# State-space stage: each unit's preparation issued one unit earlier, its splitting as a separate stream, states multiplied by C in place

## The chip, the cores and the metric

The kernel runs on one core of one Trainium2 chip. The metric is the device time of one execution in microseconds (us). Time before: 5238.29 us, the median of three runs (5235.17 to 5256.56).

The engines that matter here are PE (TensorE, matrix products), DVE (VectorE), ACT (ScalarE, activation functions) and POOL (GpSimd). SP (SyncE) issues nearly all DMA transfers. Each engine works through its own list of instructions in the order in which the program issues them; an instruction that waits for a semaphore holds up all that stand behind it on that engine.

## The reference

A stack of layers works on x of shape (4, 96, 64, 64). Layer 0 is a two-layer Mamba (selective state-space) block on the 4096 positions of each image. Layers 1 to 3 (a bilinear channel mixer, frequency-domain attention and quantised feed-forward layers) follow. The change touches layer 0 alone:

```python
def _mamba_block(seq, ln_g, ln_b, in_w, conv_w, conv_b, xproj_w, dt_w, dt_b, A_log, Dp, out_w):
    mu = seq.mean(-1, keepdims=True)
    var = ((seq - mu) ** 2).mean(-1, keepdims=True)
    h = (seq - mu) * jax.lax.rsqrt(var + EPS) * ln_g + ln_b
    xs, z = jnp.split(h @ in_w, 2, axis=-1)
    xp = jnp.pad(xs, ((0, 0), (DCONV - 1, 0), (0, 0)))
    xc = sum((conv_w[:, k] * xp[:, k:k + L, :] for k in range(DCONV))) + conv_b
    xc = jax.nn.silu(xc)
    dbl = xc @ xproj_w                       # -> dt, Bm, Cm
    delta = jax.nn.softplus(dt @ dt_w + dt_b)
    dA = jnp.exp(delta[..., None] * -jnp.exp(A_log))
    dBx = delta[..., None] * Bm[:, :, None, :] * xc[..., None]
    hstates = jax.lax.associative_scan(comb, (dA, dBx), axis=1)[1]   # h = dA*h + dBx
    y = jnp.einsum('blds,bls->bld', hstates, Cm) + Dp * xc
    return (y * jax.nn.silu(z)) @ out_w
...
for i in range(NLAYERS):                     # 2 layers, C = 96, 192 inner channels, 16 states
    seq = seq + _mamba_block(seq, ...)
```

## The kernel before, in words

`_mamba` (from line 49) computes layer 0. The positions are cut into 8 chunks of 512 (TC). A **unit** is one chunk of one layer for one pair of images, so there are 8 x 2 x 2 = 32 units; they run one after the other, ordered so that a unit's input, made by the layer below, is three units old (two units at the ends are "late": there it is younger). A unit has 24 **steps** (`NS`): three groups k of channels, four r, two halves h. A step scans 4 x 32 rows of 16 states over 512 positions, as two DVE scans of [128, 512].

Per step s, the functions that issue its work are:

- `copies(s)` (L425): a DMA that spreads delta from DRAM (`ddl`) over the states into `a`, six buffers. In 4 of 24 steps, the *apart* ones (steps 2, 6, 10 and 14 of a unit), a second one spreads delta times x into `db`.
- `broadcasts(s)` (L440): PE spreads delta times x over the states into PSUM `pq` (three buffers), from tiles `ux` and `uy`, which hold it split in two parts of fewer bits. In apart steps pq is only a place for the decays.
- `decays(s)` (L449): ACT takes exp of `a` times A, two instructions.
- `product(s)` (L454): times B (`bc`), on DVE in pq; in apart steps on POOL in db.
- `scans(s)` (L459): two DVE scans into `hs`; between them DVE does the product of step s+1. Then POOL multiplies two of the four rows of hs by C into `hc` (on L476). hs and hc have two buffers each, one for two steps (a group g).
- `states(g)` (L478): ACT copies the last column of hs, the state that this unit hands to the next chunk (`hst`).
- `reduce(g)` (L482): PE sums over the states, into `py`.
- `gate` (L492), three times per unit: DVE adds D times x, POOL multiplies by silu(z).

Beside this stream stand generators that prepare and finish units. They are advanced in slots by `Side` (L500): one slot per step (two in a few units), a generator keeps the slot sequence until it yields "free" or "gap", and lanes have an order of rank. `norm` (L189) centres and scales (its reciprocal root is 12 small POOL instructions on tiles `ra` and `r`, its result `hn` is written by DVE). `front` (L252) makes the input projection with the convolution (six matmul groups `mm_i`, one PSUM buffer `mm` for all side work), silu, `mm_dbl` and its split (`dbl`, `dh`, `dx`), the step sizes (`mm_d`, `dl`, softplus), the copy of delta to DRAM, the products `du` = delta times x, and their splitting into ux, uy and ul with DMAs that move quarters between partitions. `tail` (L359) makes the output projection `mm_o` of a finished unit and copies it, as the next layer's input `s` or, for layer 1, as `ft` to DRAM; `rest` (L405) takes the statistics of ft on DVE.

While unit n is scanned, front(n+1) runs as the highest lane from step 0, tail(n-1) is put in line at step 3, norm(n+2) at step 10, and at step 23 what is left is drained:

```python
lanes = (self.front, self.tail, [] if self.tail else self.norm, self.rest)
```

The order of the main loop in each step is: product, broadcasts and decays of an apart step s+2, broadcasts(s+2), reduce of the group that ended two steps before, slots, decays(s+3), scans(s), copies(s+5), states, gate.

Of the kernel before, what the change touches and what calls it, by code (L numbers as in the profile page):

```python
# [48 lines left out]
def _mamba(ctx, tc, io, w, fd, fstats, xsums):  # L49
# [26 lines left out]
    A, HS, HC = ("a", 0, 2, 6), ("hs", 0, 4, 2), ("hc", 0, 4, 2)  # L76
# [12 lines left out]
    out_wT = staged(io["out_wT"], "out_wT", [C, 2, 128], *HC)  # L89
# [12 lines left out]
    dtH = stage("dtH", [128, NL, 256], *HC)  # L102
# [66 lines left out]
    seq, made, ys = {}, {}, {}  # L169
    pqs, das, dbs, hss, hcs, pys = {}, {}, {}, {}, {}, {}  # L170
# [18 lines left out]
    def norm(unit):  # L189
# [47 lines left out]
        for n, b in enumerate(bs):  # L237
# [11 lines left out]
            nc.vector.tensor_tensor(hn_buf[b, l][:C, 3:], p, xc[n], ALU.mult)  # L249
            yield "free"  # L250

    def front(unit):  # L252

        ch, l, pr = unit
        bs = (2 * pr, 2 * pr + 1)
        for j in range(6):
# [13 lines left out]
            if j == 0:  # L270
                xcv = tl("xcv", unit, [128, 3, TC], bufs=2)
            if j == 3:
                zs = tl("zs", unit, [128, 3, TC], bufs=2)
# [32 lines left out]
        bcs = []  # L306
        for k in range(3):
# [8 lines left out]
            if k == 1:  # L316
                for at in range(2):
                    t = tl(f"bc{at}", unit, [128, 2, TC], bufs=2)
                    src = ddb[at].rearrange("s n t -> s (n t)")[:, None].to_broadcast([DS, 8, 2 * TC])
                    nc.sync.dma_start(t.rearrange("p n t -> p (n t)"), src)  # L320
                    bcs.append(t)
# [6 lines left out]
        us, parts, dus, cut = [], [], [], []  # L328
        made[unit] = [xcv, zs, *bcs, dd, us, parts]
        for at in range(6):  # L330
# [6 lines left out]
            for k in ((0, 1), (2,))[at] if at < 2 else ():  # L337
                dus.append(tl(f"du{k}", unit, [128, TC], to="du", bufs=3))
                nc.gpsimd.tensor_tensor(dus[k], dl[:, k, :], xcv[:, k, :], ALU.mult)
# [7 lines left out]
            while at == 3 and side.step < NS * units.index(unit) - 3:  # L347
                yield "gap"
            if 1 <= at < 4:
                cut.append([tl(f"{x}{at}", unit, [128, TC], F32R, to=x, bufs=3) for x in ("ux", "uy")])  # L350
                for t in cut[-1]:
                    nc.scalar.copy(t, dus[at - 1])
# [4 lines left out]
            yield "gap"  # L357

    def tail(unit):  # L359
# [4 lines left out]
        for n in range(2):  # L364
# [13 lines left out]
            else:  # L378
                ft = work.tile([C, TC], F32, name=f"ft_{tag(unit)}_{n}", tag="ft", bufs=2)
# [6 lines left out]
    def way_out(unit):  # L386
# [11 lines left out]
        for n in range(2):  # L398
            b = 2 * pr + n
            nc.vector.bn_stats(fstats[:, b, ch, :], po[:C, n, :])  # L400
            ft = work.tile([C, TC], F32, name=f"ft_{tag(unit)}_{n}", tag="ft", bufs=2)
# [57 lines left out]
    def scans(s):  # L459
# [3 lines left out]
        if h == 0:  # L463
            hss[g] = scan.tile([128, 4, TC], F32, name=f"hs_{name(s)}", tag="hs")
            hcs[g] = scan.tile([128, 4, TC], F32, name=f"hc_{name(s)}", tag="hc")
# [9 lines left out]
        sl = slice(2 * h, 2 * h + 2)  # L475
        (nc.gpsimd if s + 1 < n_steps else nc.vector).tensor_tensor(hcs[g][:, sl, :], hss[g][:, sl, :], bc(unit, 3, k, h), ALU.mult)  # L476

    def states(g):  # L478
        ch, l, pr = steps[2 * g][0]
        nc.scalar.copy(hst[pr, l, g % 12], hss[g][:, :, TC - 1])  # L480

    def reduce(g):  # L482
# [3 lines left out]
        hc = hcs.pop(g)  # L486
# [13 lines left out]
    class Side:  # L500
# [5 lines left out]
        def __init__(self):  # L506
            self.front, self.tail, self.norm, self.rest, self.held, self.step = [], [], [], [], None, 0

        def slot(self):
            waiting = []  # L510
            while True:
                lane = self.held
                if lane is None:
                    lanes = (self.front, self.tail, [] if self.tail else self.norm, self.rest)
# [12 lines left out]

        def drain(self):
# [4 lines left out]
    n_steps = len(steps)  # L533
    with tc.manual_schedule():
# [12 lines left out]
        for s in range(n_steps + NS):  # L547
# [5 lines left out]
            if at == 0:  # L553
                if n + 1 < len(units) and n + 1 not in late:
                    side.front += ([norm(units[n + 1])] if n == 0 else []) + [front(units[n + 1])]
                    side.norm += [weights(1)] * (n == 0)
# [997 lines left out]
```

## Time and profile before

| what | value |
|---|---|
| median of the runs | 5238.29 us (5235.17 to 5256.56) |
| profiled execution | 5239.08 us, span 5237.3 us |
| granted TensorE clock, mean | 0.819 |
| DVE busy over the span | 4322.3 us (83%) |
| PE, ACT, POOL busy | 4069.8, 2693.7, 2988.1 us |
| state-space stage, first to last scan | 93 to 3084 us |
| everything behind it | 3084 to 5237 us |

Busy time is the time in which an engine executes an instruction; waiting isn't counted. A row of the profile by lines gives the line, engine, operation and tiles (out<-in), the count, then busy us and mean ns of one, then the idle time of the engine just before these instructions with what ended it. Who ended a wait is inferred from semaphores; where an instruction waits for several, the name can be that of the wrong one.

### The profile page before, as it was taken

The numbers are of one execution on the slowest core, as the hardware profiler recorded it, in microseconds if no ns is written. First come the engines' busy times: TensorE is split into PE (matmuls) and PEld (weight loads), VectorE is DVE, ScalarE is ACT, GpSimd is POOL, SyncE is SP. The second block draws the span as 40 slices with busy tenths as digits, with TensorE's granted clock in tenths as the row PEclk, the third lists the DMA queues.
The fourth block names the chain that finished last, engine by engine and source line by source line (L and its number), as shares of the span: only waits on it lengthen the run. The fifth ranks groups of instructions, "written<-read, shape, count | busy, mean of one in ns | idle before, by whom it ended". The sixth has DMA issues, their size and how long they took to land.

```text
span 5237.3 us, 52687 instructions
## 1 busy us (share of the span) xinstructions
PE 4069.8 (78%) x15440; PEld 1747.5 (33%) x15440; DVE 4322.3 (83%) x5639; ACT 2693.7 (51%) x5149; POOL 2988.1 (57%) x2105
## 2 busy tenths in 40 slices
PE   5677777777777777777777637899898899989776
PEld 2222222222222222222222102345455555545565
DVE  2879899898989989899998887879787978787655
ACT  3565666656566665656656520024453544434566
POOL 2878888888888888888888860002130312212122
PEclk7767877777787777778787658999999999999977
DMA  4768888888887888888788765553325233332110
GB/s 100 179 168 192 197 193 205 195 197 195 197 195 192 209 196 193 195 197 202 186 208 196 175 168 157 165 174 94 95 86 155 85 98 97 100 90 79 53 33 21
DMA packets 314046, 800.19 MB, mean 153 GB/s; under 512 B 52247, under 2 KB 58106, under 8 KB 312702
## 3 DMA queue, kind: packets, MB, share of 16 engines
q1 hardware_dynamic: 310174, 790.53, 59.8%
q10 hardware_dynamic: 3584, 6.29, 0.4%
q8 instruction: 123, 2.02, 0.2%
q14 instruction: 165, 1.35, 0.1%
HBM read 703.83 MB, written 67.63 MB: 147 GB/s over the span
## 4 chain that ended last, share of the span: by engine, by line
PE 26%; DVE 24%; issue 15%; POOL 11%; ACT 9%; DMA 7%; SPq 1%; DVEq 0%; POOLq 0%; ACTq 0%
DVE hs L470 10%; PE py L895 10%; DVE pq L457 6%; DMA a<-ddl 5%; POOL hc L476 4%; PE py L488 2%; DVE z L880 2%; ACT a L452 2%; DVE a L1110 2%; PE px L1177 2%; PE ph L1092 2%; PE pa L1078 2%; PE mm_i L264 2%; POOL t L1248 1%; PE pv L1133 1%
## 5 line engine op out<-in xcount | busy, mean ns | idle before, releaser
L476 POOL TENSOR_TENSOR hc<-hs,bc 128x1024 f32<-128x1024 f32 x767 | 1803.2, 2360 | 318.4 <-DVE hs L470 305.7
L470 DVE TENSOR_TENSOR_SCAN hs<-a,hst,pq 128x512 f32<-128x512 f32 x1280 | 1575.0, 1263 | 40.1 <-ACT hst L480 17.3
L895 PE MATMUL py<-z,wk 128*96 128x512 f32 x2304 | 1113.1, 612 | 25.0 <-issue 14.0
L452 ACT ACTIVATE a<-a,aneg 128x512 f32<-128x512 f32 x1280 | 846.1, 711 | 223.4 <-DMA a<-ddl 216.1
L880 DVE TENSOR_TENSOR z<-cp,cp 128x512 f32<-128x512 f32 x1152 | 794.9, 717 | 183.7 <-PE py L895 169.0
L457 DVE TENSOR_TENSOR pq<-pq,bc 128x1024 f32<-128x1024 f32 x640 | 773.2, 1208 | 111.6 <-PE pq L447 111.5
L488 PE MATMUL py<-hc,red 128*32 128x512 f32 x3072 | 672.3, 840 | 39.4 <-POOL hc L476 39.4
L895 PEld LDWEIGHTS py<-z,wk 128*96 128x96 f32 x2304 | 366.9, 169 | 448.7 <-issue 318.9
L447 PE MATMUL pq<-uy,sel 64*128 64x512 f32 x768 | 262.9, 643 | 281.1 <-DVE hs L470 275.1
L470 DVE TENSOR_TENSOR_SCAN hs<-pq,hst,db 128x512 f32<-128x512 f32 x256 | 325.5, 1271 | 148.1 <-POOL dx L303 95.0
L1145 POOL MEMSET zz<- 96x2 f32 x16 | 1.6, 98 | 738.5 <-ACT zz L1154 738.5
L264 PE MATMUL mm_i<-hn,wk 97*128 97x512 f32 x512 | 297.7, 710 | 118.3 <-ACT xcv L275 93.2
L1246 POOL TENSOR_TENSOR o<-o,fb 128x384 f16<-128x384 f16 x64 | 67.0, 1047 | 547.1 <-ACT o L1251 544.1
L452 ACT ACTIVATE pq<-a,aneg 128x512 f32<-128x512 f32 x256 | 177.0, 692 | 343.5 <-DMA a<-ddl 249.3
L457 POOL TENSOR_TENSOR db<-db,bc 128x1024 f32<-128x1024 f32 x128 | 302.0, 2360 | 23.8 <-DMA db<-ddu 23.8
L447 PEld LDWEIGHTS pq<-uy,sel 64*128 64x128 f32 x768 | 97.9, 234 | 568.4 <-DVE hs L470 431.7
L447 PE MATMUL pq<-ux,sel 64*128 64x512 f32 x512 | 181.5, 635 | 96.4 <-DVE hs L470 76.6
L275 ACT ACTIVATE xcv<-mm_i,pvec 128x512 f32<-128x512 f32 x96 | 66.0, 687 | 313.1 <-PE mm_i L264 147.8
L1177 PE MATMUL px<-bd,a 128*96 128x128 f32 x1024 | 148.2, 293 | 67.1 <-DVE a L1110 56.2
L1146 POOL TENSOR_TENSOR zz<-zz 96x256 f32<-96x256 f32 x128 | 122.8, 959 | 133.4 <-ACT zz L1153 81.3
L264 PEld LDWEIGHTS mm_i<-hn,wk 97*128 97x128 f32 x512 | 98.7, 214 | 291.1 <-issue 165.5
L447 PEld LDWEIGHTS pq<-ux,sel 64*128 64x128 f32 x512 | 66.9, 231 | 305.3 <-DVE hs L470 212.0
(286 smaller groups left out, 6534.3 us busy)
## 6 DMA issues: line engine op xcount, KB each, us to landing
a<-ddl SPq DMA_DIRECT2D x768, 512.0 KB, 6.8
cp<-p SPq DMA_DIRECT2D x480, 192.0 KB, 2.7
db<-ddu SPq DMA_DIRECT2D x128, 512.0 KB, 9.0
bc<-ddb SPq DMA_DIRECT2D x64, 512.0 KB, 7.8
cp<-p SPq DMA_DIRECT2D x480, 64.0 KB, 2.7
ddl<-dl SPq DMA_DIRECT2D x128, 192.0 KB, 3.9
tw_k_fwd<-in_k_fwd SPq DMA_DIRECT2D x64, 256.0 KB, 3.4
tw_k_inv<-in_k_inv SPq DMA_DIRECT2D x64, 256.0 KB, 3.1
```

Of the source, the lines that this page charges most:

```text
L264: nc.tensor.matmul(p, wt[:, 0:128], hn_buf[bs[k], l][:, cols], **f)
L447: nc.tensor.matmul(pqs[s][:, i, :], sel[rows, r, :], made[unit][6][k][h][rows], start=True, stop=True)
L452: nc.scalar.activation(to[:, i, :], das[s][:, i, :], AF.Exp, scale=acol(s, i))
L457: engine.tensor_tensor(t, t, bc(unit, 2, k, h), ALU.mult)
L470: nc.vector.tensor_tensor_scan(hss[g][:, at, :], d0[:, i, :], d1[:, i, :], hst[pr, l, g % 12][:, at : at + 1], ALU.mult, ALU.add)
L476: (nc.gpsimd if s + 1 < n_steps else nc.vector).tensor_tensor(hcs[g][:, sl, :], hss[g][:, sl, :], bc(unit, 3, k, h), ALU.mult)
L488: nc.tensor.matmul(pys[unit, k][32 * (i // 2 + i % 2 * 2) :][:32], red[:, r, :], hc[:, i, :], start=(r == 0), stop=(r == 3))
L880: nc.vector.tensor_tensor(zs[n], cps[q, r0], cps[q, r1], ALU.mult)
L895: nc.tensor.matmul(pys[q], wk[k // KG][:, k % KG, :], zs.pop(n), start=(k == 0), stop=(k == NE - 1))
L1078: nc.tensor.matmul(pa[j][:, jj, :], kf[:, 2 * (j % 2) + jj, :], dd[j][:, jj, :], start=True, stop=True)
L1146: nc.gpsimd.tensor_tensor(z0[:, :, 0, :], z0[:, :, 0, :], z1[:, :, 0, :], ALU.add)
L1177: nc.tensor.matmul(p[:, j, :], a2[i % 2][:, kk, :], tabs["bd"][:, int(kk > 0), :], start=True, stop=True)
```

## The change

Three things change in `_mamba`; the rest of the kernel is the same.

First, the tile hc goes. POOL multiplies hs by C in place, all but the last of the 512 columns. ACT, after copying the last column to hst, multiplies that column by C itself, with one instruction in groups of k < 2 and two in those of k = 2. hs has three buffers for the earlier 2 + 2 of hs and hc; reduce reads hs. xcv and zs have three buffers for two, and ft uses the buffers of sq0 and sq1.

Second, front(n+2) joins a new lane `ahead` at step 4 of unit n, runs when nothing else does once norm(n+2) is through, and what is left of it goes on first thing in unit n+1 (`turn`). load and norm move from steps 8 and 10 to 2 and 4. Odd steps have two slots. The drain at step 23 is gone.

Third, the end of front becomes a generator of its own, `split`, in the highest lane `low`. It begins two steps into the unit before its own, with the copies of B and C, and is tied to steps. tail and rest now rank ahead of front and norm.

```diff
         def __init__(self):
-            self.front, self.tail, self.norm, self.rest, self.held, self.step = [], [], [], [], None, 0
+            self.low, self.tail, self.front, self.norm, self.ahead, self.rest, self.held, self.step = [], [], [], [], [], [], None, 0
...
-                    lanes = (self.front, self.tail, [] if self.tail else self.norm, self.rest)
+                    lanes = (self.low, self.tail, self.rest, self.front, [] if self.tail else self.norm, self.ahead)
...
+        def turn(self):
+
+            if self.held is self.ahead:
+                self.held = self.front
+            self.front += self.ahead
+            self.ahead.clear()
...
     def front(unit):
...
+        while unit not in normed:
+            yield "gap"
...
-                xcv = tl("xcv", unit, [128, 3, TC], bufs=2)
+                xcv = tl("xcv", unit, [128, 3, TC], bufs=3)
...
-                zs = tl("zs", unit, [128, 3, TC], bufs=2)
+                zs = tl("zs", unit, [128, 3, TC], bufs=3)
...
         dd = dp.tile([2, 32, 3, 2, TC], F32, name=f"ddl_{tag(unit)}", tag="ddl")
         for q in range(4):
             nc.sync.dma_start(dd[q % 2, :, :, q // 2, :], dl[32 * q : 32 * q + 32])
...
+        while side.low:
+            yield "gap"
+        for ks in ((0, 1), (2,)):
+            for k in ks:
+                dus.append(tl(f"du{k}", unit, [128, TC], to="du", bufs=3))
+                nc.gpsimd.tensor_tensor(dus[k], dl[:, k, :], xcv[:, k, :], ALU.mult)
+            if len(ks) == 2:
+                yield "gap"
+        side.low.append(split(unit, ddb, dus, us, parts))
+
+    def split(unit, ddb, dus, us, parts):
+
+
+        cut, start = [], NS * units.index(unit) - NS
+        while side.step < start + 2:
+            yield "gap"
+        for at in range(2):
+            t = made[unit][2 + at] = tl(f"bc{at}", unit, [128, 2, TC], bufs=2)
+            src = ddb[at].rearrange("s n t -> s (n t)")[:, None].to_broadcast([DS, 8, 2 * TC])
+            nc.sync.dma_start(t.rearrange("p n t -> p (n t)"), src)
+        yield "gap"
+        for at in range(1, 6):
+            if at > 1:
+                yield "gap"
...
-            while at == 3 and side.step < NS * units.index(unit) - 3:
+            while at < 4 and side.step < start + 8 * at - 3:
                 yield "gap"
...
     def tail(unit):
...
-                ft = work.tile([C, TC], F32, name=f"ft_{tag(unit)}_{n}", tag="ft", bufs=2)
+                ft = work.tile([C, TC], F32, name=f"ft_{tag(unit)}_{n}", tag=f"sq{n}", bufs=1)
...
     def scans(s):
...
-            hss[g] = scan.tile([128, 4, TC], F32, name=f"hs_{name(s)}", tag="hs")
-            hcs[g] = scan.tile([128, 4, TC], F32, name=f"hc_{name(s)}", tag="hc")
+            hss[g] = scan.tile([128, 4, TC], F32, name=f"hs_{name(s)}", tag="hs", bufs=3)
...
-        sl = slice(2 * h, 2 * h + 2)
-        (nc.gpsimd if s + 1 < n_steps else nc.vector).tensor_tensor(hcs[g][:, sl, :], hss[g][:, sl, :], bc(unit, 3, k, h), ALU.mult)
+        sl, LC = slice(2 * h, 2 * h + 2), TC - 1
+        (nc.gpsimd if s + 1 < n_steps else nc.vector).tensor_tensor(hss[g][:, sl, :LC], hss[g][:, sl, :LC], bc(unit, 3, k, h)[:, :, :LC], ALU.mult)
 
     def states(g):
-        ch, l, pr = steps[2 * g][0]
-        nc.scalar.copy(hst[pr, l, g % 12], hss[g][:, :, TC - 1])
+
+        unit, k, r, h = steps[2 * g]
+        ch, l, pr = unit
+        end = hss[g][:, :, TC - 1]
+        nc.scalar.copy(hst[pr, l, g % 12], end)
+        col_c = made[unit][3][:, :, TC - 1 : TC]
+        for i in (k,) if k < 2 else (0, 1):
+            e = end if k < 2 else end.rearrange("p (h i) -> p i h", i=2)[:, i]
+            nc.scalar.activation(e, e, AF.Copy, scale=col_c[:, i])
 
     def reduce(g):
...
-        hc = hcs.pop(g)
+        hc = hss.pop(g)
...
             if at == 0:
-                if n + 1 < len(units) and n + 1 not in late:
-                    side.front += ([norm(units[n + 1])] if n == 0 else []) + [front(units[n + 1])]
-                    side.norm += [weights(1)] * (n == 0)
+                side.turn()
+                if n == 0:
+                    side.front += [norm(units[1]), front(units[1])]
+                    side.norm += [weights(1)]
...
-                if at == 8:
+                if at == 2:
                     load(units[n + 2])
-                if at == 10:
+                if at == 4:
                     (side.front if n + 1 in late else side.norm).append(norm(units[n + 2]))
+                    side.ahead.append(front(units[n + 2]))
...
             side.slot()
-            if n == 0 or n + 1 in late:
+            if n == 0 or n + 1 in late or s % 2 == 1:
                 side.slot()
...
-            if at == NS - 1 and n + 1 < len(units):
-                side.drain()
```

## The prediction

> **What bounds the kernel now.** I read the page first: engine totals, then the 40 slices.
>
> ```profile
> PE 4069.8 (78%) x15440; PEld 1747.5 (33%) x15440; DVE 4322.3 (83%) x5639; ACT 2693.7 (51%) x5149; POOL 2988.1 (57%) x2105
> ...
> DVE  2879899898989989899998887879787978787655
> ...
> POOL 2878888888888888888888860002130312212122
> ```
>
> DVE leads, and in the first 23 slices POOL runs almost level with it; later POOL is nearly idle. The diff touches only that first part, so I asked for windows: the whole stage (93 to 3084 us, first scan to last) and two units in its middle.
>
> ```profile
> 93.00:3084.00 2991.00, 2207.75 (x7417) 684.10 (x7419) 2666.67 (x2366) 1782.57 (x3090) 2549.77 (x1579) 0.75 0.81 193
> 1059.20:1149.70 90.50, 67.32 (x235) 20.93 (x235) 82.66 (x74) 55.90 (x96) 78.87 (x50) 0.79 0.82 194
> 1149.70:1243.50 93.80, 71.15 (x235) 22.35 (x235) 83.92 (x76) 57.05 (x100) 81.33 (x52) 0.75 0.86 200
> ```
>
> Columns: length, then PE, PEld, DVE, ACT and POOL busy. A unit takes 92.15 us on average; DVE works 83.3 of it and POOL 80.1. So DVE idles 8.9 us per unit, which is all that a better order can win (8.9 x 32 = 285 us), and POOL has 12 us to spare per unit. Next, who ends DVE's idle time (waits of DVE in the stage), and the timeline around the longest one (sum, times, longest in us):
>
> ```profile
> DVE hs L470 <- POOL dx L303: 95.0, 28, 4.0
> DVE hn L249 <- PE mm_r L240: 71.9, 35, 11.1
> DVE pq L457 <- PE pq L447: 63.0, 40, 3.2
> DVE hs L470 <- POOL hc L476: 35.6, 30, 3.8
> DVE hs L470 <- ACT hst L480: 27.5, 9, 5.4
> ```
>
> ```profile
> 1011.17 3.61 DVE L470 TENSOR_TENSOR_SCAN hs<-a,hst,pq 128x512 f32<-128x512 f32 x3
> ...
> 1018.46 0.18 ACT L480 COPY hst<-hs 128x4 f32<-128x4 f32 x1
> ...
> 1018.73 1.28 DVE L470 TENSOR_TENSOR_SCAN hs<-pq,hst,db 128x512 f32<-128x512 f32 x1 [3.94 <-POOL dx L303]
> ```
>
> The name "POOL dx" is misleading: the scan starts 0.09 us after ACT's hst copy ends, and that copy gives back one of only two hs buffers. So the stall is ACT being late after silu, dbl and dh. It comes once per unit, at step 14 (3 to 4 us). The rest is a PE wait at step 12 (1.6 us here) and hn at steps 22 and 23 (2.3).
>
> **The change, part by part.** I count in steps; step 26 is step 2 of the next unit. A DVE step with its product lasts 3.48 us (1022.23, 1023.40, 1024.52 and 1025.71 are the starts of scan, product, scan, next scan), one before an apart step 2.36, a gate y 0.64 more. DVE's instructions keep their number and shapes, so its 83.3 us stay; only waits change.
>
> *Removed.* With three hs buffers freed by reduce(g-3) instead of hst(g-2), the scan no longer waits for the newest ACT copy: the step-14 stall (3.6) and the small ones at steps 4 and 6 (1.2) go. As front's silu moves to step 17, the step-12 wait (1.7) goes too. What is late next is below. ACT's wait of some 8 us at a unit's start (pq on a<-ddl, 249.3 us in 31 times) goes, but at steps 0 to 2 DVE shows next to no idle time, so it is worth nothing by itself. The drain at step 23 goes; only in unit 1 does DVE idle long there (13 us): take -8 in all for the five first and last units, bounds -20 and 0.
>
> *Added: a chain from silu to db(26).* The front of unit n+2 now runs through the end of unit n, and its last pieces, softplus and du0, du1, stand on POOL ahead of hc(23) and db(26). db(26) is what scan 26 reads. Worked from these rows:
>
> ```profile
> L476 POOL TENSOR_TENSOR hc<-hs,bc 128x1024 f32<-128x1024 f32 x767 | 1803.2, 2360 | 318.4 <-DVE hs L470 305.7
> L457 POOL TENSOR_TENSOR db<-db,bc 128x1024 f32<-128x1024 f32 x128 | 302.0, 2360 | 23.8 <-DMA db<-ddu 23.8
> L339 POOL TENSOR_TENSOR du<-dl,xcv 128x512 f32<-128x512 f32 x96 | 120.9, 1274 | 18.2 <-ACT dl L601 18.2
> ```
>
> ACT: table load, two silus, table load 5.5 (1089.98 to 1095.43); decays 20 and 21 2.5 (1.25 a pair back to back); states(8) 0.4. Now PE's reduce(8) waits for that states(8), because the last column's product is ACT's, and mm_dbl stands behind reduce(8): 1.5 (eight rows 1.07 to 1.93) and 2.9 (1011.77 to 1014.68). Then ACT: dbl and dh 2.0; decays 2.5; states 0.4; ux, uy 1.05; dl0 0.6 and 0.9 of waiting for reduce(9) and mm_d0; decays 1.25; dl1 0.6; decays 1.25; states 0.4; dl2 0.6; table load and softplus 2.8. That is 27.2. POOL: 2 x 1.24 + 2 x 2.33 = 7.1 (back to back). Sum 34.3 us. The table load cannot start before hc(15), reduce(7), mm_i5 and zs have passed, some 1.9 us into step 17; from there to scan 26 DVE has 8 x 3.48 + 2.36 + 0.64 - 1.9 = 28.9 us of work. DVE loses 5.4 us, part at pq(22) and pq(24), which stand behind mm_dbl and mm_d1, most at scan 26. With PE at its faster rows 1.5 less; starting at step 18, as POOL's ul2 pushes it, 2.7 more, and 1.2 more at the upper price of the added ACT instructions below. Bounds 3.9 and 9.3; I take 6.5, towards the late start, since POOL has work for every moment there.
>
> *Moved: the tail straight behind the gate.* Before, it ran at step 10, long after POOL had finished y. Now mm_o stands on PE at step 28. POOL leaves db(26) and does du2, hc(24), hc(25), hc(26), y2: 1.24 x 2 + 2.33 x 3 = 9.5 us. Then two matmuls 2.5, copy 0.56, mm_o 3.6 (3.1 to 4.4), copy 0.56: 16.7 us after scan 26. In half the units (layer 1) DVE's two bn_stats, which follow at once as `rest` moved up, ask for these copies after 11.1 us and 0.6 later: 5.1 us lost, less what scan 30 would wait anyway. In the other half pq(31) is behind mm_o and mm_xc, ready at 18.5 against 15.3: 3.2. If POOL had no backlog y2 would come 4 us sooner, and the losses would be 1 and 0. I take 3.5, bounds 0.5 and 5.
>
> *Moved: the norm, from steps 10-23 to 4-10.* ra (12 instructions, 3.4 us: 1042.37 to 1045.79) now delays hc(31), reduce(3) and mm_r. Before, hn cost 2.3 at a place where POOL had slack; here POOL runs with a backlog: from db(26) to db(38) it has 41.7 us of work against DVE's 41.5. I take 3, bounds 1.5 and 4.
>
> *Added: the last column on ACT.* 16 more small ACTIVATEs per unit. The hst rows cost ACT 0.08 to 0.1 net each (1018.46 to 1018.54): 1.4 us, already in "states 0.4" above. From above, the ve row, eight columns with a pointer operand, costs 0.3 (1035.52 to 1035.82): 4.8 us, of which six instructions, 1.2 us, lie in the chain. From below the chain is shorter by nothing, as the instructions are new. I take the hst row, the same four columns. The Trainium skill, "ScalarE: Activation LUTs", section What ACT_TABLE_LOAD costs, gives 186 ns plus 93 per pointer operand, less 93 of overlap; that would be 3.0 us per unit, and its Rules for kernel authors would put a multiplication on VectorE. By the page the chain above would be 0.6 longer; no row here shows a scale pointer on four columns. POOL's in-place product is priced by the db row, itself in place: no change. The fewer buffers for ft (xs on ACT now waits for bn_stats and the fd transfer) cost ACT 1 to 2 us at step 29, covered by its lead; without that lead, as much on DVE.
>
> **Sum.** DVE idle per unit: before 8.9; after 6.5 + 3.5 + 3 = 13.0. +4.1 us in 27 regular units is +111, -8 at the ends: +103. The profiled execution took 5239.08 us (span 5237.3), within 1 us of the median 5238.29. Forecast 5340 us. All lower bounds: 5.9 - 8.9 = -3.0 per unit, -81, -20: 5138. All upper: 18.3 - 8.9 = +9.4 per unit, +254: 5493.
>
> **Rivals.**
> *Faster: ACT keeps its lead.* Now that hs waits on ACT are gone, nothing holds DVE if softplus ends 7.1 us before DVE wants scan 26, that is 1.3 us before scan 24. Then POOL has no backlog and the tail finds y2 ready: idle 1 + 1 + 2.5 = 4.5, -4.4 x 27 - 8 = -127: 5112. For: ACT is busy only 56 us a unit and the DMA waits at the start are gone. Against: the 34 us chain above, and PE and ACT now wait for each other at every reduce.
> *No change.* Chain 5, tail 1.5, norm 2.5: 9.0, as before: 5235. For: in the unit shown the old chain from silu to its stall also cost 1.6 + 3.9.
> *POOL becomes the bound.* Its 80.1 us plus waits for ACT at ra, dx and du, without room to catch up: units of about 99 us, +6.9 x 27: 5420. Against: steps 16 to 23 still give POOL 4 us of slack.
>
> **How the numbers follow.** 0.5% is 26 us, about what a measurement here can tell: 0.95 us per unit. Forecast case (5265 to 5400) 0.58, POOL-bound or worse 0.12, no change 0.08, faster 0.22. The range 5170 to 5430 leaves out most of the faster rival's times below 5170 and the top of the upper bound, about 0.2 together. The forecast's own range is 5275 to 5400.
>
> **What would show it.** Right: DVE idle near step 2 of every unit, ended by POOL db behind du; bn_stats waiting for ft in layer-1 tails; PE's py waiting for ACT; no stall at step 14; a stage longer by 100 us while everything behind it keeps its length. Wrong: softplus ending a step earlier than my chain has it, or y2 early because POOL keeps up. Most doubtful are the PE durations, since its granted clock is 0.75 in the mean here.

## The result, and the profile after

The changed kernel takes 5685.15 us (median of four runs, 5676.99 to 5694.74), beside 5243.43 us for the kernel before in the same comparison. The ratio is 1.0841, with a 95% interval of 1.0810 to 1.0871: 441 us slower, where the forecast had said about 100. The sign was right, the time lies 255 us above the top of the range.

First the page of the changed kernel: engine totals, then DVE and POOL in 40 slices of the span.

```profile
PE 4114.3 (72%) x15440; PEld 1749.4 (31%) x15440; DVE 4329.9 (76%) x5639; ACT 2829.2 (50%) x5661; POOL 2978.6 (52%) x2105
...
DVE  2767778777777777787787787787978788786765
...
POOL 3667777777877777777777776200212112132122
```

DVE and POOL do the work they did before, but their digits in the stage have dropped from 8 and 9 to 7 and 8. ACT is busy 135 us longer than before and PE 45; DVE has 8 us more and POOL 10 less. So what DVE lost is waiting, and POOL, at 7 tenths, is not the bound. The windows of the changed kernel (length, busy time of PE, PEld, DVE, ACT, POOL, granted clock of TensorE, DMA share, GB/s) show where: the stage, two units in it, and all that lies behind it.

```profile
95.00:3527.00 3432.00, 2253.84 (x7417) 688.53 (x7417) 2674.24 (x2366) 1917.59 (x3602) 2542.98 (x1579) 0.70 0.69 168
1534.86:1644.16 109.30, 72.40 (x239) 22.75 (x235) 84.21 (x77) 61.32 (x117) 79.93 (x51) 0.70 0.70 170
1644.16:1746.37 102.21, 69.75 (x239) 22.02 (x235) 82.93 (x75) 60.18 (x113) 79.79 (x51) 0.72 0.73 172
3527.00:5687.00 2160.00, 1819.40 (x7928) 1043.67 (x7924) 1649.32 (x3264) 884.63 (x2021) 416.69 (x434) 0.92 0.33 101
```

The stage runs from 95.0 to 3526.5 us: 3431.5 us instead of 2990.1, which is the whole difference. What follows takes 2160 us as against 2154. Units now alternate between about 102 and 109 us (90.5 and 93.8 before). Adding up the idle gaps of DVE between the first and the last scan gives 758 us against 324: 433 more. Units 6 to 28 have 22.2 us each against 8.8, which makes 307 of the 433; units 3 to 5 and 29 make 58, and the five at the ends 68.

Who ends DVE's waits, and PE's, in the stage (sum, times, longest in us):

```profile
DVE pq L473 <- PE pq L463: 324.7, 122, 9.4
DVE hn L249 <- PE mm_r L240: 151.2, 31, 8.9
DVE hs L485 <- POOL db L473: 125.7, 40, 4.5
DVE fstats L424 <- ACT ft L396: 67.2, 29, 3.2
...
```

```profile
PE py L510 <- ACT hs L502: 598.4, 206, 8.9
PE pq L463 <- DVE hs L485: 331.6, 182, 4.9
```

The old first line, the scan waiting under the name of "POOL dx", is gone: the stall at step 14 has disappeared as forecast. In its place DVE waits for PE, and PE for ACT. At 206 of the 384 reduces PE stood still, 598 us in all, for an instruction of 0.3 us on four columns.

How that happens, in one unit: first ACT, then PE, then POOL, and the scan at the end (start, duration, engine, line, operation, tiles; in brackets the idle time ahead of it).

```profile
1829.52 0.59 ACT L281 COPY zs<-mm_i 128x512 f32<-128x512 f32 x1 [3.02 <-PE mm_i L271]
1830.12 1.28 ACT L283 ACT_TABLE_LOAD   x1
1831.41 1.48 ACT L283 ACTIVATE xcv<-xcv 128x1536 f32<-128x1536 f32 x1
1832.81 1.47 ACT L284 ACTIVATE zs<-zs 128x1536 f32<-128x1536 f32 x1
1834.29 1.28 ACT L468 ACT_TABLE_LOAD   x1
1835.59 2.56 ACT L468 ACTIVATE a<-a,aneg 128x512 f32<-128x512 f32 x4
1838.05 0.18 ACT L498 COPY hst<-hs 128x4 f32<-128x4 f32 x1
1838.32 0.48 ACT L502 ACTIVATE hs<-hs,bc 128x2 f32<-128x2 f32 x2
1843.46 0.59 ACT L297 COPY dbl<-mm_dbl 128x512 f32<-128x512 f32 x1 [4.65 <-PE mm_dbl L294]
```

```profile
1838.72 2.07 PE L510 MATMUL py<-hs,red 128*32 128x512 f32 x8 [7.90 <-ACT hs L502]
1840.71 1.69 PE L291 MATMUL mm_dbl<-xcv,xp 128*64 128x512 f32 x4
1842.33 1.08 PE L294 MATMUL mm_dbl<-xcv,xp 64*64 64x512 f32 x4
```

```profile
1845.52 1.27 POOL L307 TENSOR_TENSOR dx<-dbl,dh 128x512 fp32r<-128x512 f32 x1 [8.70 <-ACT dh L301]
...
1858.97 2.49 POOL L332 TENSOR_TENSOR du<-dl,xcv 128x512 f32<-128x512 f32 x2 [2.79 <-ACT dl L637]
1861.42 2.34 POOL L491 TENSOR_TENSOR hs<-hs,bc 128x1022 f32<-128x1022 f32 x1
1863.72 2.34 POOL L473 TENSOR_TENSOR db<-db,bc 128x1024 f32<-128x1024 f32 x1
```

```profile
1866.10 1.28 DVE L485 TENSOR_TENSOR_SCAN hs<-pq,hst,db 128x512 f32<-128x512 f32 x1 [4.39 <-POOL db L473]
```

ACT reaches the state copy and the last column only after 5.5 us of table loads and silus and 2.5 us of decays. PE, whose reduce waits for it, is held for 7.90 us, with mm_dbl and the pq of coming steps behind it. ACT then waits 4.65 us for mm_dbl, and POOL 8.70 us for ACT. The chain ends at db(26) and scan 26 starts at 1866.10, 4.39 us late. PE waits for ACT at the reduce, and ACT for PE at mm_dbl, with POOL and DVE behind them. This mutual wait is called the ring below.

### The profile page after: what moved, and what is told of

Its sections match the earlier page's. It is cut to its first block, busy times and chain, and to the rows that moved or that the text cites. A ratio compares the mean times of both kernels' runs of the same rounds, so it can differ in the third digit from the quotient of the medians.

```text
span 5686.9 us, 53763 instructions
## 1 busy us (share of the span) xinstructions
PE 4114.3 (72%) x15440; PEld 1749.4 (31%) x15440; DVE 4329.9 (76%) x5639; ACT 2829.2 (50%) x5661; POOL 2978.6 (52%) x2105
## 5 line engine op out<-in xcount | busy, mean ns | idle before, releaser
L491 POOL TENSOR_TENSOR hs<-hs,bc 128x1022 f32<-128x1022 f32 x767 | 1798.0, 2356 | 332.2 <-DVE hs L485 324.6
L510 PE MATMUL py<-hs,red 128*32 128x512 f32 x3072 | 726.9, 921 | 677.5 <-ACT hs L502 598.4
L463 PE MATMUL pq<-uy,sel 64*128 64x512 f32 x768 | 242.6, 626 | 326.0 <-DVE hs L485 325.9
L510 PEld LDWEIGHTS py<-hs,red 128*32 128x32 f32 x3072 | 104.1, 128 | 885.0 <-issue 537.5
L307 POOL TENSOR_TENSOR dx<-dbl,dh 128x512 fp32r<-128x512 f32 x32 | 40.5, 1267 | 292.9 <-ACT dh L301 292.9
L463 PE MATMUL pq<-ux,sel 64*128 64x512 f32 x512 | 157.6, 610 | 22.9 <-DMA ux<-ul 17.2
## 6 DMA issues: line engine op xcount, KB each, us to landing
bc<-ddb SPq DMA_DIRECT2D x64, 512.0 KB, 12.8
```

The costliest lines, as they stand in the source:

```text
L463: nc.tensor.matmul(pqs[s][:, i, :], sel[rows, r, :], made[unit][6][k][h][rows], start=True, stop=True)
L510: nc.tensor.matmul(pys[unit, k][32 * (i // 2 + i % 2 * 2) :][:32], red[:, r, :], hc[:, i, :], start=(r == 0), stop=(r == 3))
```

## The experiments

Seventeen runs, each with its ratio to the kernel before in the same comparison. "Against before" is that ratio, less one, times 5243 us; "before" or "after" in a name says which of the two kernels the run starts from. The intervals of e1, e2, e4 and e17 reach 23 to 36 us to either side, the others less, and a smaller difference between two runs says nothing.

| run | time (us) | ratio, 95% interval | against before |
|---|---|---|---|
| changed kernel | 5685.15 | 1.0841 [1.0810, 1.0871] | +441 |
| e1 after, no column | 5393.63 | 1.0289 [1.0229, 1.0349] | +152 |
| e2 before, in place | 5322.83 | 1.0154 [1.0095, 1.0213] | +81 |
| e3 before, in place, no column | 5201.33 | 0.9937 [0.9915, 0.9960] | -33 |
| e4 after, rest last | 5683.79 | 1.0842 [1.0799, 1.0885] | +441 |
| e5 before, state on POOL | 5248.87 | 1.0006 [0.9996, 1.0016] | +3 |
| e6 after, state on POOL | 5415.85 | 1.0319 [1.0303, 1.0335] | +167 |
| e7 = e6, norm late | 5617.05 | 1.0702 [1.0676, 1.0728] | +368 |
| e8 = e6, norm and tail late | 5355.20 | 1.0202 [1.0182, 1.0221] | +106 |
| e9 after, column aside | 5432.43 | 1.0354 [1.0330, 1.0379] | +186 |
| e10 before, three hs, norm moved | 5232.63 | 0.9973 [0.9957, 0.9989] | -14 |
| e11 = e2, states first | 5249.99 | 1.0006 [0.9995, 1.0016] | +3 |
| e12 after, states first | 5571.56 | 1.0625 [1.0607, 1.0643] | +328 |
| e13 before, three hs, norm kept | 5180.01 | 0.9883 [0.9859, 0.9906] | -61 |
| e14 = e6, layer-1 tail later | 5486.08 | 1.0442 [1.0408, 1.0477] | +232 |
| e15 = e6, front at home | 5713.33 | 1.0890 [1.0865, 1.0915] | +467 |
| e16 after, front at home | 5888.16 | 1.1217 [1.1190, 1.1244] | +638 |
| e17 = e8, front at home | 5473.47 | 1.0452 [1.0384, 1.0520] | +237 |

Theory after the first look at the traces: PE's reduce now waits for ACT in every group, and this ring is the loss. The rival: the order of the streams (front ahead, tail and norm early) is the loss, and PE's waits for ACT only stand where others would.

### e1 to e4: the ring or the order

e1 takes the product out of the changed kernel:

```diff
         nc.scalar.copy(hst[pr, l, g % 12], end)
-        col_c = made[unit][3][:, :, TC - 1 : TC]
-        for i in (k,) if k < 2 else (0, 1):
-            e = end if k < 2 else end.rearrange("p (h i) -> p i h", i=2)[:, i]
-            nc.scalar.activation(e, e, AF.Copy, scale=col_c[:, i])
```

> The changed kernel without ACT's product on the last column of hs (that column of y is then not multiplied by C): reduce no longer waits for ACT. Theory A (coupling): most of the 447 us lost come from PE standing still at reduce until ACT has made that product (598 us of such waits in the trace). Then mm_dbl starts some 5 us sooner, the db stall at step 2 and the pq stalls at steps 21 and 23 go (11.7 us per unit), the tail's and hn's shrink by 2: about 13.5 us in 27 units, 5320 us. Theory B (order): the place of du, tail, rest and norm makes the loss and POOL's backlog keeps it; only ACT's own 5 us of small instructions per unit go and 3 to 4 us are won: 5590 us.

e2 puts the in-place product, the three hs buffers and ACT's column into the kernel before and leaves its order alone:

```diff
-            hss[g] = scan.tile([128, 4, TC], F32, name=f"hs_{name(s)}", tag="hs")
-            hcs[g] = scan.tile([128, 4, TC], F32, name=f"hc_{name(s)}", tag="hc")
+            hss[g] = scan.tile([128, 4, TC], F32, name=f"hs_{name(s)}", tag="hs", bufs=3)
...
-        hc = hcs.pop(g)
+        hc = hss.pop(g)
```

> The kernel before with the in-place product alone (three hs buffers, no hc, ACT's copy and product of the last column), in the old order of the streams. Theory A: the coupling is harmful by itself: reduce waits for ACT, whose hst copy ends 2.3 us after hc in the median before, and the old chain from silu to dbl stands behind it: 4 to 8 us per unit more, 5380 to 5500 us. Theory B: the third hs buffer takes away the step-14 stall and the coupling is hidden: 3 to 5 us per unit less, 5090 to 5140 us.

e3 is e2 without the product, the same lines removed as in e1.

> As e2, but without ACT's product of the last column (that column of y is then not multiplied by C), so that reduce waits for POOL alone and hs has three buffers. Both theories: the step-14 stall (3.6 us) and the ones at steps 4 and 6 (1.2) go: -4.8 us x 28 units, 5105 us. If the 3.6 us only move to the next wait (PE or POOL), 5200 to 5240 us.

Measured: +152, +81 and -33 us. So the ring, with ACT's time for the product, costs 441 - 152 = 289 us in the new order and 81 + 33 = 114 in the old one, and the new order without it costs 152 + 33 = 185. Both theories hold a part, and the ring is the larger. e3 also answers a point of the forecast: the removed wait for an hs buffer brought 33 us, where I had credited 3.6 + 1.2 us in each of 27 units. The wait at step 14 fell from 3.4 to 0.6 us, but those for pq at steps 6 and 12 grew by 0.4 and 0.9.

e4 ranks `rest` last again in the changed kernel:

```diff
-                    lanes = (self.low, self.tail, self.rest, self.front, [] if self.tail else self.norm, self.ahead)
+                    lanes = (self.low, self.tail, self.front, [] if self.tail else self.norm, self.ahead, self.rest)
```

> The changed kernel with the lane rest (bn_stats) ranked last again, the rest unchanged. Theory B in its simple form: the 4.5 us at step 4 of each layer-1 tail go: 14 x 4.5 = 63 us less, 5625 us. Theory A: the same stall comes back two steps later at pq behind mm_o and mm_xc, as in the layer-0 tails (3.2 us): 5665 us.

No change (1.0842). The wait of bn_stats at step 4 of every second unit (4.6 us, units 6 to 28) is gone, and in the same units the waits at steps 6, 7 and 9 have grown, by 5.0 us in all (3.3, 5.0 and 5.8 for 0, 3.6 and 5.2, with 0.4 less at step 8). The early rank of bn_stats costs nothing by itself. At steps 6 and 7 DVE waits for a pq from PE.

### e9, e11, e12: ACT's time, or its place in the queue

e9 keeps all of ACT's work and takes only PE's wait away. The product goes to a tile that nobody reads:

```diff
-            nc.scalar.activation(e, e, AF.Copy, scale=col_c[:, i])
+            to = wp.tile([128, 4], F32, name=f"aside_{g}_{i}", tag="aside")
+            nc.scalar.activation(to[:, : 4 if k < 2 else 2], e, AF.Copy, scale=col_c[:, i])
```

> The changed kernel with all of ACT's work for the last column kept, but written to a small tile of its own that nobody reads, so the last column that PE reduces is not multiplied by C and PE waits for ACT's product no more. Theory A (PE's wait for ACT in the middle of its queue is what costs the 291 us): near the version without these instructions, 5394, plus at most their 1.8 us in the chain per unit: 5395 to 5455. Theory B (the 16 instructions of 0.30 us on ACT, 4.8 us a unit, are what costs): 5550 to 5690.

+186 us, so 255 of the 289 us come from PE's wait. The other 34 us are what ACT's time can cost; they are about the uncertainty of e1. PE's longest waits in the stage of e9:

```profile
PE pq L463 <- DVE hs L485: 521.4, 224, 4.9
PE mm_xc L203 <- ACT xc L197: 85.1, 23, 13.7
PE mm_d L314 <- ACT dl L318: 58.6, 27, 2.8
```

PE is back at waiting for DVE, that is, ahead of it.

e11 and e12 move the state copy and the product to the start of the even step, ahead of that step's decays and side work, in e2 and in the changed kernel:

```diff
+            if s % 2 == 0 and 0 < s <= n_steps:
+                states(s // 2 - 1)
             if s + 2 < n_steps:
                 unit, k, r, h = steps[s + 2]
...
-            if s % 2 == 0 and 0 < s <= n_steps:
-                states(s // 2 - 1)
```

> The in-place version in the old order (5323), with ACT's state copy and last-column product moved to the start of the same even step, ahead of that step's decays and side work. Theory A (PE waits because the product stands behind decays in ACT's queue): PE's 222 us of waiting for it fall by more than half, and the time to 5215 to 5260. Theory B (the product is late because the scan before it is, and now the decays stand behind it): 5310 to 5400, with DVE waiting for decays.

> The changed kernel with the same move: state copy and product at the start of the even step. Theory A (place in ACT's queue): most of the 291 us that the coupling costs come back, 5430 to 5530. Theory B (any wait of PE for ACT costs this much): 5640 to 5700.

In the old order this gives back 78 of the 114 us (+81 to +3). In the new one it gives back 113 of 289, and a part of the ring stays; PE's waits in the stage of e12:

```profile
PE pq L463 <- DVE hs L485: 338.3, 163, 5.1
PE py L510 <- ACT hs L502: 255.5, 64, 7.0
```

The waits fell from 206 to 64, but those that remain are long, 4.0 us in the mean. In units 6 to 28 they stand at two places, but for 1.0 us: at step 20 (126.7 us), where ACT is still busy with the table loads and the silus, and at step 22 (74.0), behind dbl and dh, for which ACT had to wait. At step 1, where PE waits 75.6 us for ACT in the changed kernel, it now waits 41.6 us for POOL. A place at the start of the step can't avoid work that stands ahead on ACT from earlier steps. Both of my numbers for e12 missed: the place matters, and is not all.

### e5 and e6: the ring taken out in a kernel that computes everything

POOL copies the state column itself just ahead of its product and then multiplies all 512 columns; ACT no longer touches hs:

```diff
-        sl, LC = slice(2 * h, 2 * h + 2), TC - 1
-        (nc.gpsimd if s + 1 < n_steps else nc.vector).tensor_tensor(hss[g][:, sl, :LC], hss[g][:, sl, :LC], bc(unit, 3, k, h)[:, :, :LC], ALU.mult)
+        sl = slice(2 * h, 2 * h + 2)
+        engine = nc.gpsimd if s + 1 < n_steps else nc.vector
+        engine.tensor_copy(hst[pr, l, g % 12][:, sl], hss[g][:, sl, TC - 1])
+        engine.tensor_tensor(hss[g][:, sl, :], hss[g][:, sl, :], bc(unit, 3, k, h), ALU.mult)
```

> The order of before, the product with C in place over all 512 columns, three hs buffers; the state column is copied to hst by POOL just ahead of its product, two columns per step, and ACT's copy is gone, so ACT no longer touches hs. Theory A (what cost 121 us in the in-place version of before was only that PE's reduce waited for ACT): POOL gets 24 small copies a unit, 2.4 to 6.8 us by the ra row (12 in 3.4 us) as the upper price, and has 12 us to spare, so 5190 to 5220, as the version without the last column (5201) and no PE wait on ACT for hs. Theory B (POOL has no room at its small grain, each copy delays db and the next product): DVE waits for POOL db and hc, 5260 to 5300.

> The changed kernel with the state column copied by POOL ahead of an in-place product over all 512 columns; ACT touches hs no more, and every column is multiplied by C. Theory A (the coupling of PE and ACT costs 291 us of the 447, the order of the streams the rest): as the version without the last column, 5394, plus at most 30 for POOL's copies in the chain to db: 5385 to 5425. Theory B (POOL is the bound in the new order): 24 copies of 0.1 to 0.28 us lengthen each unit by 2.4 to 6.8 us, 5470 to 5610.

e6 at +167, between e1 and e9, confirms them in a complete computation. e5 came out at +3, between its two theories: POOL's 768 copies take 0.187 us each (143 us of POOL's time) and cost 36 us of e3's gain. The order alone is worth 167 - 3 = 164 us here.

### e7, e8, e14 to e17: what in the order costs the 164 us

All but e16 start from e6. e7 moves load and norm back to steps 8 and 10, and e8 moves the tail to step 10 as well:

```diff
-                if at == 2:
+                if at == 8:
                     load(units[n + 2])
-                if at == 4:
+                if at == 10:
                     (side.front if n + 1 in late else side.norm).append(norm(units[n + 2]))
```

> The run before it (state on POOL, new order), with the norm of unit n+2 and its x load back at steps 10 and 8 of unit n; the chain behind it moves with it, some six steps later. Theory A (the norm's place and the chain's end cost their stalls, 5.0 us a unit at hn and 1.8 at scan 26): both fall, hn to about 2.5, and the time falls by 90 to 130 against that run, to about 5290. Theory B (a stall taken away only comes up at the next wait, as with the bn_stats): within 25 us of that run.

> The run before it, with the tail of unit n-1 at step 10 of unit n as well, in the units without a late norm. Theory A (bn_stats and pq behind the early tail cost about 4 us a unit): another 80 to 110 less, near 5200. Theory B (what bn_stats loses comes back behind it): within 25 us of the run with the late norm alone.

Both theories fell for e7: the late norm made it 201 us slower than e6. The timeline of PE in the first steps of a unit of e7 shows one of the new waits:

```profile
1700.22 0.79 PE L463 MATMUL pq<-uy,sel 64*128 64x512 f32 x2 [3.49 <-DVE hs L485]
1700.95 1.93 PE L501 MATMUL py<-hs,red 128*32 128x512 f32 x8
1702.81 2.02 PE L385 MATMUL mm_o<-y,of_w 128*96 128x512 f32 x2
1704.82 2.02 PE L386 MATMUL mm_o<-y,of_w 64*96 64x512 f32 x2
1706.76 2.02 PE L387 MATMUL mm_o<-s,fus_w 96*96 96x512 f32 x2
1709.46 2.02 PE L385 MATMUL mm_o<-y,of_w 128*96 128x512 f32 x2 [0.67 <-ACT ft L396]
1711.41 2.02 PE L386 MATMUL mm_o<-y,of_w 64*96 64x512 f32 x2
1713.36 2.02 PE L387 MATMUL mm_o<-s,fus_w 96*96 96x512 f32 x2
1716.05 0.79 PE L314 MATMUL mm_d<-dx,dt_w 24*128 24x512 f32 x1 [0.67 <-ACT ft L396]
1716.77 0.79 PE L463 MATMUL pq<-uy,sel 64*128 64x512 f32 x2
```

The front came later by as much as the norm, and its end (mm_dbl, mm_d) now falls where the tail runs. Between one pq and the next PE has 16.6 us of reduce, mm_o and mm_d, and DVE, which takes 3.48 us per step, waits 5.0 us for that pq, at step 6 of every unit from 6 to 28. The waits of the scans at steps 2 and 10 and the one for hn have also grown, by 2.4, 3.4 and 1.9 us per unit. With the tail moved too (e8) the wait for pq at step 6 is gone: 262 us less than e7, which neither theory had, and 61 less than e6.

e14 puts only the tails of layer 1 later, at step 7, with ft in the place of the layer's stored input:

```diff
-                else:
+                elif units[n - 1][1] == 0:
                     side.tail.append(tail(units[n - 1]))
+            if at == 7 and 0 < n < len(units) and n + 1 not in late and units[n - 1][1] == 1:
+                side.tail.append(tail(units[n - 1]))
```

> The new order with the state on POOL (5416), with the tails of layer 1 alone at step 7 instead of 3 (ft takes the place of the layer's stored input). Theory A (the bn_stats that wait for ft 4.9 us in these units are a cost of their own): 5335 to 5375. Theory B (they come back at the next wait for PE, as when their rank was changed): 5395 to 5435.

Both theories fell again: 65 us slower than e6. The bn_stats wait did not go, it moved to step 8 and grew from 4.9 to 7.2 us in those units. In the units between them, whose tails had not moved, the wait at step 6 grew from 3.5 to 8.1 us. I did not follow these waits further back.

e15 keeps the front from starting early in e6, e16 does so in the changed kernel, e17 in e8 (with the tail at step 9):

```diff
-                    lanes = (self.low, self.tail, self.rest, self.front, [] if self.tail else self.norm, self.ahead)
+                    lanes = (self.low, self.tail, self.rest, self.front, [] if self.tail else self.norm)
```

> The new order with the state on POOL (5416), with the front of a unit not started before the unit ahead of it begins, as in the old order; tail and norm stay early. Theory A (the front ahead costs what the late tail and norm did not bring back, 106 us): 5290 to 5330. Theory B (early tail and norm cost it): 5390 to 5430. Theory C (front and tail then meet on PE, as with the late norm): 5480 to 5650.

> The changed kernel itself with that one part undone: the front does not start a unit ahead. Theory A (the chain through the coupled reduces is the largest term, 11.7 us a unit against 6.5 forecast): 5330 to 5450. Theory B (the coupling stops the chain wherever it runs, and tail and front meet on PE): 5600 to 5800.

> The version with the state on POOL and late tail and norm (5355), with the front of a unit not started before the unit ahead of it begins (the tail at step 9, not 10). All three then stand about at their old times, under the new ranking and with the split as a stream of its own. Theory A (the front ahead costs what is left over the old order): 5240 to 5290. Theory B (the front's place costs nothing once tail and norm are late): 5330 to 5380. Theory C (at home the front is done too late under the new ranking, as with early tail and norm): 5450 to 5700.

| against before | front ahead | front at home |
|---|---|---|
| tail and norm early | +167 (e6) | +467 (e15) |
| tail and norm late | +106 (e8) | +237 (e17) |

e16 says the same with the ring: +638 against +441. e15 and e16 lie above every range that was expected for them, e17 in its third. So the front running a unit ahead, the part of the change that I had blamed most, is not what costs: under the new ranking it saves 131 to 300 us. Early tail and norm cost 61 us where the front is ahead and 230 where it isn't. The numbers do not add over the parts, since each part decides which others it meets on PE. In e17 the norm comes behind the front again, and the wait for hn has moved to step 17, 8.7 us per unit.

What stays open: e8 is still 103 us above e5, with tail and norm at their old times. DVE's longest wait in the stage of e8 shows where part of it stands:

```profile
DVE hs L485 <- POOL db L473: 180.7, 63, 4.7
```

e5 has 13.5 us of it. In e8 it comes at steps 6 and 10, 3.1 and 3.4 us per unit; there, in the unit that I read, POOL does dx and three du ahead of db. What brings this about is not shown. The front ahead, the new ranking of the lanes, the second slot in odd steps and the split as a stream of its own are left as candidates. Of the ranking only the place of `rest` was tried by itself (e4), and of the others only the front.

### e10 and e13: the third hs buffer by itself

Both give the kernel before three hs buffers beside two of hc. The room comes from one decay buffer less and from ft. In e10 ft shares with the squares, as in the change, and `rest` has to stand ahead of the norm for it; in e13 ft takes the place of the layer's stored input, which mm_o has just read for the last time, and no instruction changes its place:

```diff
-    A, HS, HC = ("a", 0, 2, 6), ("hs", 0, 4, 2), ("hc", 0, 4, 2)
+    A, HS, HC = ("a", 0, 2, 5), ("hs", 0, 4, 3), ("hc", 0, 4, 2)
...
-                ft = work.tile([C, TC], F32, name=f"ft_{tag(unit)}_{n}", tag="ft", bufs=2)
+                ft = work.tile([C, TC], F32, name=f"ft_{tag(unit)}_{n}", tag=f"s{b}")
...
-        das[s] = scan.tile([128, 2, TC], F32, name=f"a_{name(s)}", tag="a", bufs=6)
+        das[s] = scan.tile([128, 2, TC], F32, name=f"a_{name(s)}", tag="a", bufs=5)
...
-            hss[g] = scan.tile([128, 4, TC], F32, name=f"hs_{name(s)}", tag="hs")
+            hss[g] = scan.tile([128, 4, TC], F32, name=f"hs_{name(s)}", tag="hs", bufs=3)
```

> The kernel before with hs in three buffers beside two of hc, so that only the number of hs buffers differs in the stream of products; the room comes from one decay buffer less (five of a) and from ft sharing a tile with the squares, with the two bn_stats moved ahead of the norm. Theory A (the third buffer is worth the 36 us that the in-place version without the column showed, no matter how it is got): 5195 to 5220, and no stall at step 14. Theory B (ACT's shorter lead over the scans gives the gain back): 5240 to 5300, with DVE waiting for ACT's decays. My forecast had priced this buffer at 3.6 + 1.2 us a unit, 5085 to 5110.

> The kernel before with three hs buffers beside two of hc, and every instruction in its old order: the room comes from one decay buffer less and from ft taking the place of the layer's stored input, which is read for the last time just before it. Theory A (the run with the norm behind the two bn_stats lost its gain at hn, 6.5 to 6.9 us at step 23 in half the units, against 2 before): 5185 to 5215, and hn back at 2. Theory B (one decay buffer less is what holds it back): 5220 to 5245, with ACT waiting for decays' transfers as in that run.

e10 gives -14 us: the stall at step 14 is gone, but hn waits 4.1 us at step 23 in the mean (1.9 before). e13 gives -61 us, ratio 0.9883 (0.9859 to 0.9906). It is the fastest version found, 1.2% below the kernel before. Its DVE waits for PE and hn, and its stage:

```profile
DVE pq L457 <- PE pq L447: 156.0, 113, 9.4
DVE hn L249 <- PE mm_r L240: 91.4, 45, 14.2
...
DVE hs L470 <- POOL db L457: 8.0, 2, 4.5
```

```profile
91.00:3030.00 2939.00, 2205.12 (x7419) 658.35 (x7421) 2665.40 (x2366) 1784.72 (x3091) 2549.56 (x1579) 0.76 0.80 196
```

Of the three long lines of waits for hs before (95.0, 35.6 and 27.5 us) none is left. In their place DVE waits more for pq: 156 us, where it was 63. Idle per unit falls by 2.2 us, from 8.8 to 6.6: a stall that is taken away comes up in part at the next wait.

## Why the prediction was right in sign and wrong in size

Idle time of DVE per unit by the places that the forecast named (units 6 to 28, mean; e1 beside it):

| term | forecast, bounds | changed kernel | e1, no ring |
|---|---|---|---|
| chain to db(26), steps 20 to 26 | 6.5 (3.9 to 9.3) | 11.3 | 2.8 |
| tail, steps 4 to 8 | 3.5 (0.5 to 5) | 5.8 | 5.2 |
| norm, hn | 3 (1.5 to 4) | 5.0 | 5.0 |
| sum | 13.0 | 22.2 | 13.0 |

The chain itself, from the table load of silu on, set against the working of the forecast (us; units 6 to 28, mean):

| | forecast | changed kernel | e1, no ring |
|---|---|---|---|
| start of the table load | 1.9 into step 17 | 3.0 into step 18 | 2.3 into step 18 |
| from there to the copy of dbl | 12.8 | 13.4 | 8.0 |
| from there to the end of db(26) | 34.3 | 36.0 | 27.9 |
| DVE's work in that time | 28.9 | 24.7 | 25.3 |
| DVE idle | 5.4, taken as 6.5 | 11.3 | 2.6 |

- **Removed: the stall, as forecast, but its gain too large.** There is no idle time at steps 12 and 14 any more. But the same buffer in the old order is worth 33 to 61 us (e3, e13), not 27 x 4.8 = 130.
- **The chain: the step that failed first, by its start.** The chain runs as drawn, with "PE's reduce(8) waits for that states(8)" in it, and is 1.7 us longer than its sum. What failed is "some 1.9 us into step 17; from there to scan 26 DVE has ... 28.9 us of work". The table load starts in step 18 in all 23 units, and DVE has 24.7 us of work left, 4.2 less. My upper bound let the start slip by 2.7. In the unit shown zs waits 3.02 us for the last mm_i, which PE runs behind a pq and reduce(7). Without the ring (e1) the start is nearly as late, so that comes from the order; why the front is late in the other units was not followed.
- **The ring: priced inside the chain, and nowhere else.** The wait of reduce(8) is in the sum: dbl 12.8 us behind the table load, where e1 has 8.0. For the rest I had its sentence, "PE and ACT now wait for each other at every reduce", as an argument against the faster rival, and gave it no price. In all the ring is worth 289 us (e1), of which 255 are PE's waits (e9). In DVE's idle time that is 8.5 us per unit in the chain, 0.6 at the tail, none at hn, and 70 us in the nine units outside 6 to 28.
- **ACT's small instruction.** I took the hst row, 0.08 to 0.1 us net, against 0.3 from the ve row. The groups of the changed kernel by shape:

```profile
L502 ACT ACTIVATE hs<-hs,bc 128x4 f32<-128x4 f32 x256 | 77.3, 302 | 23.8 <-ACT hst L498 0.8 <-POOL hs L491 0.4 <-issue 0.4
L498 ACT COPY hst<-hs 128x4 f32<-128x4 f32 x384 | 69.8, 182 | 15.9 <-DVE hs L485 15.9
L502 ACT ACTIVATE hs<-hs,bc 128x2 f32<-128x2 f32 x256 | 62.4, 290 | 11.8 <-ACT hst L498 0.7
```

The upper price was right: 0.29 to 0.30 us. What they cost by themselves is small, about 34 us (e9 against e1). The Trainium skill, "ScalarE: Activation LUTs", section What ACT_TABLE_LOAD costs, gives 186 ns plus 93 for a pointer operand plus 0.833 per column, which is an estimate of 0.28 us for four columns or two. The trace agrees within 0.02 us.

- **Tail and norm: the places right, the sizes above the bounds** (5.8 and 5.0 against 5 and 4). In units with a tail of layer 0 the wait at pq(31) is 3.2 us, as worked out. In those with a tail of layer 1 bn_stats lose 4.6, near the 5.1 worked out, but DVE then waits 4.0 more for pq at steps 7 and 8, which the forecast had allowed for the other half of the units alone. e1 has nearly the same in sum, so this is the order and not the ring. Why hn costs 5.0 and not 3 was not followed.
- **The ends: -8 forecast, +68 measured.** Units 3 to 5 and 29 make another +58, where the forecast had 4.1 each. e1 has +26 and +31, so 70 of these 126 us go with the ring.
- **The sum.** Of the 330 us of idle time that the forecast lacked, the chain makes 110, the tail 53, the norm 46, the ends 76 and units 3 to 5 and 29 42. No single term explains it. That e1 has just the 13.0 us per unit that I had forecast is chance: its terms differ from mine in both directions.
- **The rivals.** POOL did not become the bound: it is busy 2543 of 3432 us, less of the stage than before. The faster case needed ACT to keep its lead; even without the ring (e6) the kernel is 167 us slower than before. I had put the front ahead down as the cause; e15 to e17 show that it helps under the new ranking.

## What to carry to other kernels

Instructions of 0.3 us, 16 in a unit, cost some 250 us here because one engine waited for them in the middle of its queue: before a product is divided between engines, ask what stands ahead of the small part on its engine (here table loads and decays, 8 us) and what stands behind the instruction that waits for it. Price such a wait at each place where it occurs, with the longest thing ahead of it, and not by its own duration. Side work that is moved must be looked at by whom it meets in the new place, and parts of a change in order do not add up: the norm moved back alone cost 201 us, and together with the tail it brought 61, while one more buffer, with every instruction left in its place, brought more than any new order tried here.

## What was not expected of the hardware

The granted clock of TensorE differed between kernels that issue the same matmuls. It was 0.75 in the stage before, 0.70 in the changed kernel, and 0.65 in e7, where a pair of mm_o matmuls took 2.02 us. Stage windows of e7, e8 and e2 (the clock is the third number from the end):

```profile
96.00:3473.00 3377.00, 2511.16 (x7413) 722.63 (x7417) 2669.62 (x2366) 1753.08 (x2707) 2677.14 (x2346) 0.65 0.70 171
```

```profile
95.00:3193.00 3098.00, 2233.46 (x7408) 670.83 (x7409) 2668.13 (x2365) 1745.49 (x2707) 2675.67 (x2346) 0.75 0.77 186
```

```profile
92.00:3173.00 3081.00, 2363.49 (x7413) 725.41 (x7417) 2669.20 (x2366) 1916.88 (x3602) 2544.25 (x1579) 0.70 0.79 187
```

PE's busy time rises from 2233 us in e8 at 0.75 to 2511 in e7 at 0.65, though at 0.70 it is 2363 in e2 and 2254 in the changed kernel. So a part of what an order costs can be slower matmuls, and these runs do not separate it from the waiting. The clock alone does not make the 441 us: e2, at the same 0.70 as the changed kernel, loses 81.

The Trainium skill, "TensorE: Matmul & The Clock Gate", section HAM oscillation — how this bites in real kernels, advises against idle gaps of PE above about 3.4 us. Counted in the stages of these traces, such gaps number 97 in e7 and 94 in the changed kernel, but 73 in e8 at 0.75 and only 21 in e2 at 0.70. Their number does not order the clocks here, and what does was not found.
